# Second layer's weights split early and parked in DRAM, image product packed into one fp32r product, last batch closed in two parts, slot and opening order changed

## The chip, the cores and the metric

The kernel runs on one core of a Trainium2 chip. Five engines work side by side, each through its own instructions in order: TensorE (PE, with its weight loads PEld), VectorE (DVE), ScalarE (ACT), GpSimd (POOL) and SyncE (SP, which here only issues DMA transfers; ACT issues a few too). The metric is the device time of one execution in microseconds (us). Times of the runs are of the whole execution; the span in the profile goes from the first to the last instruction.

## The reference: what is computed

Two cross-attention layers on 16 sequences of 256 positions with 320 channels (20 heads of 16), against a context of 256 tokens with 512 channels. Everything is float32.

```python
def layer0(x, ctx):                       # text = first 77 tokens, ip = the other 179
    q, k, v = x @ Wq, text @ Wk, text @ Wv
    text_out = softmax(q_h @ k_h.T * scale) @ v_h
    ip_k, ip_v = ip @ Wk_ip, ip @ Wv_ip
    text_probs = softmax(q @ k.T * scale)              # over all channels
    sem = (text_probs @ text) @ ip.T * scale
    ip_probs = softmax(q_h @ ip_k_h.T * scale + 0.5 * sem) * spatial_mask
    return (text_out + ip_probs @ ip_v_h) @ Wout + bout + x

def layer1(x, ctx):                       # text = first 252 tokens, ip = the last 4
    q, k_t, v_t = heads(x @ W_q), heads(text @ W_k), heads(text @ W_v)
    probs_t = softmax(q @ k_t.T * scale)
    text_out = probs_t @ v_t
    qsem = l2norm(probs_t @ text)                      # one vector per head
    sem = qsem @ l2norm(ip).T
    probs_ip = softmax(q @ k_ip.T * scale + 0.5 * sem) * spatial_mask
    return (text_out + probs_ip @ v_ip) @ W_out + b_out + x
```

## The kernel before

**Numbers.** A matmul of fp32r operands (rounded floats) is one record in the profile, one of f32 operands is two. To keep float32 accuracy most operands are held as a high half (the rounded value, copied by ACT) and a low half (the rest, subtracted by DVE or POOL), made by `halves` (lines 187 and 188). `prod` (line 260) then adds high x high, high x low and low x high. A few products are plain f32.

**Slots.** Each layer has 80 slots: 16 batches with 5 groups of 4 heads. Slot k of layer 0 (`slot0`) computes transposed scores T for slot k, the plain scores S of slot k+2 (for the row maxima) and the weighted values of slot k-1; slot k of layer 1 (`slot1`, from slot 80 on) does the same through `both1` (lines 917 and 922), then the norms that `l2norm` needs, `norm1` (lines 975 to 980: a Gram matrix times the rounded probabilities, multiplied with the probabilities' parts on DVE and summed on DVE or POOL), for slot k-1, and the text values `attend1` (lines 988 and 990) for slot k-2, with the settling `settle1` (lines 1040 to 1048) that transposes and scales them.

The maximum of each query's scores goes in as one more row of the queries: DVE reduces (line 923), TensorE turns the maxima into a row (`maxima1`, line 955), ACT copies it (line 957) and issues a small DMA into the stacked queries `qs` (line 959).

**Pieces between.** Whatever is not tied to a slot (keys `k0`/`k1`, values, Gram matrices `t1`, queries `q0`/`o1`, the closing products `c0`/`c1`, the image softmax `i1`, the second layer's weights `w1` to `w8`) is a generator, called a task, and `STEPS` lists at which time, in slots relative to its batch, each of its steps is issued. `fill(now)` issues the steps that are due. `late` puts DVE work off while `hold` is on, until `release` or `settled`.

**Order.** What is issued in the opening (`begin`) and in layer 1 is kept in that order on all engines; in layer 0 that holds for TensorE, and the other engines' order comes from a scheduler; `queued` and `anchor` tie single instructions behind the slot's main ones.

**Stages** in the profile: loads and opening to about 82 us, layer 0 in its steady form to about 555, the transition (second layer's weights, first keys and queries of layer 1, last slots of layer 0) to about 700, layer 1 steady to about 1430, the end to 1476.5.

**Second layer's weights** (`weights7`, `weights6`, `weights2`, `weights4`): 20 parts are loaded into `rawc`, split by ACT and DVE into `wA`, `wB`, `wC`, `wE` and `wF`, all in the transition. `weights8` fills `spread_d`, a DRAM table from which each batch reads its image values `vb`.

**Image softmax and closing** (`image_softmax`, lines 1058 to 1100; `close1`): for a batch whose five groups have settled, small operations of POOL, DVE and ACT compute `probs_ip` for all heads at once into `pip`; DVE turns it into `pT` (line 1100); `close1` multiplies it with `vb` (line 1108, f32), adds the text part on DVE (line 1109), makes halves (`ho`), and `project` (line 632) multiplies with `W_out`. The last batch's image softmax is already cut once, groups 0 to 3 and group 4, but only before the turn.

## Time and profile before

| what | us |
|---|---|
| runs | 1479.34, 1482.8, 1478.5 (median 1479.34) |
| profiled execution | 1478.29 |
| its span | 1476.5 |
| layer 0, steady (157.4 to 555) | 397.6 |
| transition (555 to 700) | 145.0 |
| layer 1, steady (700 to 1430) | 730.0 |
| end (1430 to 1476.5) | 46.5 |

The mean granted TensorE clock is 0.992 of full speed. In the profile a row of the groups names line, engine, operation, the tile written and the tiles read, the shapes and the count, then busy time and mean duration in ns, then the idle time of the engine just before, with what ended it. A row of the waits says which engine at which line waited for which other: total, times, longest. A row of the chain of waits has start, length and what ran. A row of an issue has the shortest, median and longest duration in ns. PE is busy while a matmul is under way, so a busy PE isn't a PE without overlap.

### The profile page before, as it was taken

The page shows a single profiled execution, that of the slowest core. Times are in us where ns is not written, and L with a number is a line of the kernel's source. Part 1 is how long each engine was busy: PE and PEld are TensorE (multiplying, and loading weights), DVE is VectorE, ACT ScalarE, POOL GpSimd, SP SyncE. Part 2 cuts the span into 40 slices and gives each one's busy share as a digit, 9 for nine tenths or more (in the row PEclk, how much of TensorE's full clock was granted, in tenths as well). Part 3 has the DMA queues.
Part 4 walks back from the last instruction along what each step waited for, and adds up shares of the span by engine and source line. Part 5 has one row for each costly group of instructions (what it writes and reads, how often), then busy time and mean ns, then how long its engine had stood idle before and what let it go on. Part 6 is the DMA issues. An engine that isn't in the chain of part 4 may idle for free.

```text
span 1476.5 us, 35304 instructions
## 1 busy us (share of the span) xinstructions
PE 1431.7 (97%) x12438; PEld 1184.3 (80%) x12438; DVE 1167.9 (79%) x2569; ACT 955.8 (65%) x2074; POOL 1154.1 (78%) x1173
## 2 busy tenths in 40 slices
PE   6899999999999999899999999999999999999998
PEld 6788888888888878677778888888888888888865
DVE  5477776777767787977888888888888888888897
ACT  5567676767676776756666666656665666566563
POOL 5259797978787878987788878787778877887786
PEclk9899999999999999999999999999999999999999
DMA  6766666565656577665434433543454345434511
GB/s 198 170 171 178 149 158 165 152 167 147 170 151 170 149 187 215 146 184 163 135 107 140 147 117 102 161 146 102 119 161 143 93 130 160 133 100 120 150 31 50
DMA packets 230667, 211.78 MB, mean 143 GB/s; under 512 B 56314, under 2 KB 217116, under 8 KB 230492
## 3 DMA queue, kind: packets, MB, share of 16 engines
q1 hardware_dynamic: 229232, 208.57, 50.5%
q8 instruction: 99, 1.62, 0.5%
q10 hardware_dynamic: 1260, 0.97, 0.2%
q14 instruction: 76, 0.62, 0.1%
HBM read 122.07 MB, written 86.44 MB: 141 GB/s over the span
## 4 chain that ended last, share of the span: by engine, by line
PE 87%; DVE 5%; DMA 2%; ACT 2%; issue 2%; POOL 2%; SPq 1%; DVEq 0%; ACTq 0%; POOLq 0%
PE X L260 22%; PE X L975 17%; PE X L632 11%; PE P L833 7%; PE S L772 6%; PE P L988 5%; PE T L917 5%; PE T L795 5%; PE S L922 3%; PE P L990 2%; PE X L690 1%; PE X L1108 1%; POOL wt L966 1%; PE X L780 1%; SPq L83 1%
## 5 line engine op out<-in xcount | busy, mean ns | idle before, releaser
L801 POOL TENSOR_TENSOR P<-P,rs 128x512 f32<-128x512 f32 x320 | 414.4, 1319 | 142.2 <-ACT P L798 142.0
L975 PE MATMUL X<-ctb,gm 128*128 128x512 f32 x1120 | 292.2, 403 | 0.0
L966 POOL TENSOR_TENSOR wt<-P,ctb 128x512 f32<-128x512 f32 x212 | 268.5, 1295 | 0.0
L923 DVE TENSOR_REDUCE mn<-S 128x4 fp32r<-128x1008 f32 x160 | 192.8, 1205 | 80.3 <-PE S L922 78.5
L975 PEld LDWEIGHTS X<-ctb,gm 128*128 128x128 f32 x1120 | 201.2, 188 | 48.7 <-issue 0.4
L798 ACT ACTIVATE P<-T 128x512 f32<-128x512 f32 x320 | 174.7, 593 | 97.6 <-PE T L795 80.0
L978 DVE TENSOR_TENSOR wt<-X,wt 128x512 f32<-128x512 f32 x240 | 159.3, 680 | 4.0 <-PE X L975 3.4
L929 ACT ACTIVATE P<-T 128x512 f32<-128x512 f32 x212 | 115.0, 597 | 54.4 <-PE T L917 41.8
L980 POOL TENSOR_TENSOR wt<-wt 128x512 f32<-128x512 f32 x80 | 103.6, 1295 | 57.5 <-DVE wt L978 57.5
L774 DVE TENSOR_REDUCE mn<-S 128x4 fp32r<-128x716 f32 x160 | 142.4, 890 | 0.0
L965 ACT ACTIVATE ctb<-P 128x512 fp32r<-128x512 f32 x212 | 122.2, 625 | 30.4 <-PE X L975 29.2
L833 PE MATMUL P<-P,vr 128*32 128x256 f32 x1920 | 123.9, 389 | 0.6 <-DVE sp L693 0.6
L632 PE MATMUL X<-hq,wE 128*128 128x256 f32 x768 | 111.4, 290 | 4.9 <-ACT hq L615 3.6
L260 PE MATMUL X<-cta,wA 128*128 128x252 f32 (+3 forms) x726 | 104.9, 290 | 6.1 <-ACT wA L187 5.3
L632 PEld LDWEIGHTS X<-hq,wE 128*128 128x128 f32 x768 | 102.2, 196 | 7.6 <-ACT hq L615 4.0
L632 PE MATMUL X<-ho,wF 128*128 128x256 f32 x768 | 106.6, 285 | 0.9 <-DVE ho L871 0.6
L260 PEld LDWEIGHTS X<-cta,wA 128*128 128x128 f32 (+1 forms) x726 | 94.8, 191 | 10.2 <-ACT wA L187 5.6
L632 PEld LDWEIGHTS X<-ho,wF 128*128 128x128 f32 x768 | 98.7, 189 | 3.9 <-DVE ho L871 1.0
L844 DVE STREAM_TRANSPOSE nt<-P 128x512 f32<-128x512 f32 x80 | 57.1, 714 | 44.6 <-PE P L833 44.4
L833 PEld LDWEIGHTS P<-P,vr 128*32 128x32 f32 x1920 | 55.4, 111 | 41.4 <-issue 5.5
L773 DVE TENSOR_REDUCE mn<-S 128x4 fp32r<-128x308 f32 x160 | 74.4, 465 | 17.4 <-PE S L772 16.9
L917 PEld LDWEIGHTS T<-qs,ks 49*128 49x128 f32 x640 | 50.3, 184 | 46.5 <-issue 19.9
(223 smaller groups left out, 3319.6 us busy)
## 6 DMA issues: line engine op xcount, KB each, us to landing
qd<-q SPq DMA_DIRECT2D x48, 384.0 KB
kd<-kst SPq DMA_DIRECT2D x66, 256.0 KB
rawc<-in_cT_dram SPq DMA_DIRECT2D x60, 256.0 KB
qs<-qd SPq DMA_DIRECT2D x160, 96.0 KB
ks<-kd SPq DMA_DIRECT2D x160, 96.0 KB
qs<-qd SPq DMA_DIRECT2D x60, 192.0 KB
ks<-kd SPq DMA_DIRECT2D x60, 192.0 KB
qd<-q SPq DMA_DIRECT2D x32, 256.0 KB
```

What stands on the lines that cost most here:

```text
L260: last = mm(out, lhs(a, k), rhs(b, k), start=i == 0, stop=i == len(terms) - 1)
L632: mm(pp, w(s, k, slice(m * 128, (m + 1) * 128)), a[:, t], start=i == 0, stop=i == len(terms) - 1)
L774: anchor(nc.vector.tensor_reduce(mn[:, t, 1], sp[:, :, T0:], axis=AX.X, op=ALU.max))
L798: exp = anchor(nc.scalar.activation(pt, st[p], AF.Exp, scale=SCALE))
L801: anchor(nc.gpsimd.tensor_mul(pt, pt, rs[:, t : t + 1].to_broadcast([128, 2, S])))
L833: mm(pv[32 * s : 32 * s + 32, o : o + S], v[:, vt, h : h + 32], P[k, s // 2][:, t, s % 2], start=vt < 2, stop=vt != 1,)
L917: mm(st[u][:, j], c[1][rows, j, lo : lo + 128], c[0][rows, j], start=True, stop=True)
L923: anchor(nc.vector.tensor_reduce(maxes[k + 2][:, t], sp[:, :, :T1], axis=AX.X, op=ALU.max))
L965: nc.scalar.activation(R[k, u][:, t], P[k, u][:, t], AF.Copy, scale=0.5)
L966: anchor(nc.gpsimd.tensor_sub(W[k, u][:, t], P[k, u][:, t], f(R[k, u][:, t])))
L975: mm(yp, gm[:, gb], R[k, u][:, kt], start=i == 0, stop=i == len(blocks[n]) - 1)
L978: nc.vector.tensor_mul(product, yp, w[:, n])
```

## The change

1. *Weights parked.* A new task `prep` reads the 20 parts of the second layer's weights during layer 0 (slots 8.4 to 14.4 of each ten, 12 steps in ten slots), splits each (POOL copies, DVE subtracts) and stores both halves in DRAM (`parked`). In the transition the same steps only bring halves back, one DMA for a part.
2. *Packed image product.* `probs_ip` is packed as [high, low, high] and the image values as rows [high, high, low], so that one fp32r matmul with 128 rows gives what the f32 one gave. The image softmax has three more steps: high copies, low subtraction, three turns and three copies to `pT`. `vipd` has three parts, `spread_d` is ordered by position first, and its 24 fills carry three parts each.
3. *Order in a slot of layer 1.* The row of maxima is made right behind `both1(k, 1)`, for slot k+1, in the second half of the bank that holds the text sums; its DMA is issued at once. Late work is released after the first norm product and held again at once; the roundings `rounded1` move one place back. All `STEPS` of layer 1 differ.
4. *Last batch.* `close_first` closes groups 0 to 3 and starts the output product, `close_last` adds group 4 and writes the output in three transfers. In the last slot the norm parts are summed by TensorE (more `zone` matmuls) in place of the adds.
5. *Opening.* `begin` issues single steps in another order, and `opening` is the new slot 0; `queued` ties nothing before `begin` has ended.

```diff
     def queued(inst, *behind):
         for other in behind or [anchors.get(inst.ins.engine)]:
-            if other is not None:
+            if other is not None and begun:
...
+    def stored(name, w_d, kt, n, half=None, columns=False):
+        d = parked[name] = dram.tile([128, 2, kt, n], F32, name=f"parked_{name}")
...
+        for i, (part, hi, lo) in enumerate(parts):
...
+            dma(raw, part)
+            yield
+            queued(nc.gpsimd.tensor_copy(high.bitcast(FR), raw))
+            queued(nc.vector.tensor_sub(raw, raw, high))
+            if half is not None and i == 2:
+                queued(nc.vector.tensor_scalar_mul(raw, raw, half))
+            yield
+            dma(hi, high)
+            dma(lo, raw)
+            yield
...
+    def brought(parts):
+        for w, d in parts:
+            dma(w, d)
+            yield
...
     def weights7():
         cip = w1["cip"]
-        image, wki1 = by_column(wki1_d)
-        _, text, w1["k"] = by_row(wk1_d, "wA")
-        yield from in_turn(image + text, 0.3, "rawc")
+        image, wki1 = from_columns("ki")
+        text, w1["k"] = from_rows("k", "wA", 4, CP)
+        yield from brought(image + text)
...
-                    src = vipd.rearrange("(b n) c -> b n c", n=NIP)[:, :, lo : lo + 16]
-                    dma(spread_d[:, 32 * s + row : 32 * s + row + NIP, lo : lo + 16], src)
+                    dma(rows[s, :3, row : row + NIP * B, lo : lo + 16], table[:, :, lo : lo + 16])
...
-    def maxima1(k):
-        mn = maxes[k]
-        mp = bank()
+    def maxima1(k, bank):
         for t in range(2):
-            mm(mp[:4, t * 128 : (t + 1) * 128], mn[:, t], ident_r, start=True, stop=True)
+            mm(bank[:4, S + t * 128 : S + (t + 1) * 128], maxes[k][:, t], ident_r, start=True, stop=True)
         mt = buf("mt", [8, S], FR)[:4]
-        nc.scalar.copy(mt, mp[:4, :S])
+        nc.scalar.copy(mt, bank[:4, S:])
         row = QK[k][0].rearrange("(u p) j t -> u p j t", u=2)[:, XROW]
-        late(lambda: nc.scalar.dma_start(f(row), f(mt)))
+        nc.scalar.dma_start(f(row), f(mt))
...
         if k > NS + 1:
             yield lambda: summed.append(attend1(k - 2))
-        yield release
         yield lambda: both1(k, 1)
+        yield lambda: maxima(k + 1, summed)
         if last:
             yield lambda: norm1(last, 0, 0)
         yield 0.2
+        yield release
+        if mine:
+            yield hold
         for parts in summed:
             yield lambda: settle1(*parts)
         if last:
             yield lambda: norm1(last, 0, 1)
-        if mine:
-            yield lambda: rounded1(k, 0)
         yield 0.4
         if last:
             yield lambda: norm1(last, 1, 0)
-        yield 0.6
+        if mine:
+            yield lambda: rounded1(k, 0)
         if last:
             yield lambda: norm1(last, 1, 1)
-        if mine:
-            yield hold
+        yield 0.6
+        yield 0.8
+        yield lambda: stacks(k + LEAD)
         if mine:
             yield lambda: rounded1(k, 1)
-        yield 0.8
-        yield lambda: maxima(k + 2)
-        yield lambda: stacks(k + LEAD)
         yield 1.0
...
+        for d, x in pieces:
+            (nc.vector.tensor_copy if lo else nc.scalar.copy)(d[:, :, :, :8], x)
+            nc.scalar.copy(d[:, :, :, 16:24], x)
+        yield
+        for d, x in pieces:
+            pool.tensor_sub(d[:, :, :, 8:16], x, f(d[:, :, :, :8]))
+        yield
+        turned = w1["turned"]
+        for i in turns:
+            late(lambda i=i: nc.vector.transpose(turned[i], f(packed[i // 2][:, i % 2]).rearrange("p f c -> p (f c)")))
+        yield
+        settled()
+        for i in turns:
+            nc.scalar.copy(pT[i], turned[i])
         return pT, vb
+
+    def close_first():
...
+        for p in range(2):
+            row(p)
+            yield
...
+    def close_last():
...
+        for m, pp in enumerate(outs):
+            for s in range(2):
+                mm(pp, wo[1](s, 2, slice(m * 128, (m + 1) * 128)), hl[:, 2], start=False, stop=s == 1)
...
         def rows(p, hp):
-            mm(hp, bd[:, p * 128 : (p + 1) * 128], pT, start=True, stop=True)
+            mm(hp, bd[:, p * 128 : (p + 1) * 128], pT[p], start=True, stop=True)
             nc.vector.tensor_add(hp, hT[:, p], hp)
...
-        "k1": (-7, -6.2, -6.2, -5, -4.2, -3.4,),
-        "t1": (-3.2, -2.2, -2.2, -1.4, -0.2,),
-        "o1": (-7, -6.8, -6, -5.8, -4, -3.4,),
-        "i1": (6.8, 7.6, 7.6, 8.8, 9.4, 9.6, 10.6, 10.8, 10.8, 12.2,),
+        "k1": (-6.8, -5.8, -5.8, -5.2, -4.2, -3.2,),
+        "t1": (-2.6, -2, -1.2, -0.8, 0.6,),
+        "o1": (-6.8, -6.2, -5.4, -5.4, -4.6, -3.4,),
+        "i1": (7.4, 8, 8.2, 8.4, 10.2, 10.2, 10.8, 10.8, 10.8, 11.6, 12, 12.4, 12.4,),
         "c1": (12.8, 12.8, 13.4, 14, 14, 15.8,),
...
+    task(("prep",), [10 * (i // PREP) + 8.4 + 6.0 / PREP * (i % PREP) for i in range(60)], prepare)
...
     def begin():
-        parts = lambda *keys: [step(key) for key in keys if key in tasks]
-        k0, q0, s0, m0, q1 = ("k0", 0), ("q0", 0), ("s0", 0), ("m0t", 0), ("q0", 1)
-        parts(k0, k0, k0, q0, q0, q1, q0, q0, q0)
...
+        part("k0", 0)
+        part("q0", 0)
+        part("k0", 0)
...
+        score0(0, 0)
+        part("k0", 0)
+        part("v0", 1)
+        score0(0, 1)
+        part("v0", 1)
+        maxima0(0, nc.sync)
+        part("k0", 1)
...
+    def opening():
+        yield lambda: turned0(0, 1)
+        yield lambda: score0(2, 0)
...
```

278 lines of the change are left out of this document (206 added, 72 removed), and 35 rows, old and new, of the table STEPS.

## The prediction

> **What bounds the kernel now.** I read the page first, then a table of stretches, the chain of waits, the waits by line, and short timelines.
>
> ```profile
> span 1476.5 us, 35304 instructions
> PE 1431.7 (97%) x12438; PEld 1184.3 (80%) x12438; DVE 1167.9 (79%) x2569; ACT 955.8 (65%) x2074; POOL 1154.1 (78%) x1173
> ...
> PE 87%; DVE 5%; DMA 2%; ACT 2%; issue 2%; POOL 2%; SPq 1%; DVEq 0%; ACTq 0%; POOLq 0%
> ```
>
> TensorE is busy 97% and is 87% of the chain that ends last, so there are two ways to gain: less TensorE work, or fewer of its waits. The stretches say where the waits lie (columns: length; busy time of PE, its weight loads, DVE, ACT, POOL; granted clock; DMA share; GB/s).
>
> ```profile
> 48.70:81.45 32.75, 25.80 (x163) 22.36 (x161) 18.23 (x34) 13.62 (x33) 11.35 (x9) 0.79 0.54 148
> 157.40:555.00 397.60, 393.60 (x3717) 339.07 (x3709) 290.27 (x697) 288.46 (x624) 329.54 (x292) 1.00 0.62 160
> 555.00:700.00 145.00, 134.54 (x1267) 110.72 (x1267) 114.96 (x259) 96.09 (x207) 120.32 (x112) 0.99 0.64 178
> 603.90:608.60 4.70, 4.64 (x37) 2.56 (x37) 1.74 (x4) 4.09 (x9) 3.76 (x5) 0.64 0.16 44
> 700.00:1430.00 730.00, 727.27 (x6120) 585.05 (x6119) 626.55 (x1301) 455.43 (x985) 581.50 (x629) 1.00 0.42 126
> 1430.00:1476.50 46.50, 38.38 (x274) 27.39 (x274) 35.77 (x85) 17.73 (x41) 30.95 (x44) 0.99 0.16 47
> ```
>
> Busy time times clock is work at full clock. The late opening (48.7 to 81.45) holds 25.80 x 0.79 = 20.4 us of it, so 12.4 of its 32.75 us are lost. The transition loses 145 - 134.54 x 0.99 = 11.8, the end 46.5 - 38.38 x 0.99 = 8.5. Layer 0 (157 to 555) and steady layer 1 (700 to 1430) lose 4.0 and 2.7 in all: there only less TensorE work helps.
>
> **The change, part by part.**
>
> *Packed image product.* The product that adds the image tokens' part to a closed batch (line 1108) is f32 now and fp32r after, with three rows of high and low halves in place of one. A query or output product (line 632) is an fp32r matmul of the same 256 columns, so the price of the new form has a row.
>
> ```profile
> 1001.91 0.59 PE L1108 MATMUL X<-rs,rs 128*128 128x256 f32 x2
> ...
> 1042.51 1.02 PE L1108 MATMUL X<-rs,rs 128*128 128x256 f32 x4
> ```
>
> Those are two stretches of TensorE's timeline (start, length, records). The chain of waits has the fp32r groups beside them:
>
> ```profile
> 1000.26 1.81 PE X L975 x7
> ...
> 1005.65 2.91 PE X L632 x24
> ...
> 1039.22 3.45 PE X L975 x14
> ...
> 1043.54 3.16 PE X L260 x24
> ...
> 1049.90 1.82 PE X L975 x7
> ```
>
> Four records take 1.02 and two 0.59, so they start (1.02 - 0.59)/2 = 0.215 apart. One batch has 6 (3 products, two passes each): 1.29 us. Three fp32r matmuls at 2.91/24 = 0.121 are 0.36. Saved: 0.93 a batch, 14.8 over 16. Against it stand, per batch, two more transposes on DVE, seven small copies on ACT and two subtractions on POOL.
>
> ```profile
> L923 DVE TENSOR_REDUCE mn<-S 128x4 fp32r<-128x1008 f32 x148 | 178.4, 1206 | 77.3 <-PE S L922 75.4
> ...
> L978 DVE TENSOR_TENSOR wt<-X,wt 128x512 f32<-128x512 f32 x224 | 148.5, 680 | 1.2 <-PE X L975 0.8
> ...
> L980 DVE TENSOR_TENSOR wt<-wt,X 128x512 f32<-128x512 f32 x74 | 50.8, 687 | 2.5
> ...
> L939 DVE COPY sr<-S 128x16 f32<-128x16 f32 x148 | 24.2, 163 | 0.0
> ...
> L1040 DVE STREAM_TRANSPOSE nt<-P 128x256 f32<-128x256 f32 x74 | 32.5, 439 | 0.0
> ...
> L957 ACT CAST mt<-X 4x256 fp32r<-4x256 f32 x75 | 26.4, 352 | 0.3 <-PE X L955 0.3
> ...
> L895 DVE SCALAR_TENSOR_TENSOR xc<-X,bo,xc 128x256 f32<-128x256 f32 x40 | 18.0, 476 | 0.0
> ```
>
> A batch lasts 1049.90 - 1000.26 = 49.64. DVE is busy 626.55/730 of it, 42.6; with 2 x 0.439 it is 43.5 of 48.7. On the mean that is covered by idle time; in one slot it is not. Per batch the fillers are 84 key, value and Gram matmuls (3.16/24 = 0.132 each: 11.1), 48 query and output ones (5.8) and the 1.29, so the fixed part of a slot is (49.64 - 18.2)/5 = 6.3. The new times of the pieces (STEPS) leave one slot in five with 12 key matmuls alone: 6.3 + 1.6 = 7.9 us on TensorE. DVE needs there two reductions (2.41), two copies (0.33), four norm products (2.72), a sum (0.69), the settling transpose (0.44), and reciprocal, scaling and two further pieces, each between 0.16 and 0.48 by these rows (0.6 to 1.9): 7.2 to 8.5. So that slot is a tie, and behind it the late DVE work that is now released before the settling, not ahead of it, can hold a norm product's bank. Bounds for this loss: 0 (the bank ring and the next, longer slots take it up) and 2.7 us a batch (0.7 carried out of the short slot, 0.5 where ACT's copies stand behind the transposes and the exponentials behind them, 1.5 where three late pieces of 0.48 stand before the settling). I take 0.4, nearer to nothing, as DVE's mean slack is 5 us a batch. Layer 1: -14.8 + 16 x 0.4 = -8 (from -15 to +28).
>
> *Row of maxima (line 955 on).* The product that turns the maxima of a slot's scores into a row, and the small load that puts this row under the queries, come one slot later than before: in the middle of slot k for slot k+1, where it was at the end of slot k for k+2. T of slot k+1 (line 917) reads that row. Behind the second half of the scores ACT still has a pair of exponentials (2 x 0.6 us, the rounding of line 929), then the 0.352 copy, the issue and the landing:
>
> ```profile
> L929 ACT ACTIVATE P<-T 128x512 f32<-128x512 f32 x198 | 107.5, 596 | 49.1 <-PE T L917 36.6 <-PE S L922 11.4 <-ACT mt L957 0.6
> ...
> L959 ACTq DMA_DIRECT2D qs<-mt x80: 517/518/536, 669.8 to 1439.6; - x80
> ...
> 460.00 2.10 DMA kd<-kst
> ...
> 597.11 4.25 DMA rawc<-in_wvi_dram
> ```
>
> 1.2 + 0.35 + 0.52 + 2.1 (the lower of the two landings shown; this one has 4 KB, so that neither is nearer in kind, and it moves beside steady traffic as the keys of the 2.1 do) = 4.2. TensorE has 3.45 (14 norm matmuls) + 1.6 to do meanwhile in the short slot: 0.9 us to spare, more in the others. I take nothing; with a landing of 4.25 it would be 1.3 a batch. The product goes into the free half of the bank of the text sums, so that DVE's settling now also waits for ACT's copy, with that slot's norm products queued behind it: 1.2 + 0.35 after the scores, while DVE has the second reduction (1.21) and a late piece to do, so again nothing, and at most the 0.35 of the copy (inside the 2.7).
>
> *Second layer's weights.* 20 copies (ACT) and 20 subtractions (DVE) leave the transition; layer 0 takes them on POOL and DVE, with 40 stores.
>
> ```profile
> L188 DVE TENSOR_TENSOR wB<-rawc,wB 128x512 fp32r<-128x512 f32 x6 | 7.0, 1159 | 0.2 <-ACT wB L187 0.2
> ...
> L187 ACT CAST wB<-rawc 128x512 fp32r<-128x512 f32 x6 | 3.6, 623 | 1.4 <-DMA rawc<-in_wvi_dram 1.4
> ...
> L188 POOL TENSOR_TENSOR cta<-rawc,cta 128x512 fp32r<-128x512 f32 x6 | 7.7, 1294 | 0.0
> ...
> L801 POOL TENSOR_TENSOR P<-P,rs 128x512 f32<-128x512 f32 x320 | 414.4, 1319 | 142.2 <-ACT P L798 142.0
> ...
> PE X L709 <- ACT sp L705: 4.2, 2, 2.9
> ```
>
> In the transition 20 x at most 1.16 = 23 us leave DVE (115 of 145 busy) and 20 x at most 0.62 = 12 leave ACT. The costliest stall, 2.9 us at TensorE behind ACT, and the half clock behind it (0.64 over 603.9 to 608.6) start with the 4.25 us landing on which ACT's copy of wB blocks: that goes, since the halves land ready for TensorE and no engine stands between. Waits on DVE shrink; the one on spread_d below and those on POOL stay. Halves are twice the bytes, 8.2 MB in place of 4.1: 28 GB/s more beside 178. I take half of the 11.8 lost: -6 (from -10, little left, to +3, the larger loads late). In layer 0, a fifth of the stretch from 157 to 555 takes four parts: POOL 4 x at most 1.29 = 5.2 of (397.60 - 329.54)/5 = 13.6 idle, DVE 4 x 1.16 = 4.6 of 21.5. If each of 20 parts pushed a softmax product back by one such copy with no slack, 26; POOL's own idle before line 801, 142 us over 320, says it is nearer to 0: +1. SP's queue gets 60 more issues there; DMA's share is 0.62.
>
> *Opening.* The loads of contexts 2 and 3 are issued 18 places earlier on SP's queue, no longer behind the stack loads and the first maxima rows, and scores, weights and keys are interleaved anew.
>
> ```profile
> 55.66 2.32 issue
> ...
> 60.50 4.92 DMA raw<-in_cT_dram
> ...
> 67.78 3.10 DVE ctb L188 x2
> ```
>
> That load and the two splits behind it, 8.0 us of the chain, come off it; the next arrivals are the keys' round trip and the maxima, already 2.3 us of issue. I take -6 (from -12, all of the loss, to +3, a load now ahead of one that is needed sooner). The Trainium skill, "TensorE: Matmul & The Clock Gate", part 1, says that an idle window of about 3.4 us halves the clock. The row: at 603.9 an idle 2.9 did. By the page, gaps kept short would also return the clock's part, 25.80 x 0.21 = 5.4, which -12 would include; by the row it takes gaps below 2.9, and I leave -6.
>
> *End.* The last batch's image softmax goes in two parts, its output products of groups 0 to 3 are summed early, and the output leaves in three transfers.
>
> ```profile
> 1466.76 1.16 PEld L1108 LDWEIGHTS X<-rs,rs 128*128 128x128 f32 x6 [1.23 <-DVE rs L1100]
> ...
> 1469.17 3.13 PE L632 MATMUL X<-ho,wF 128*128 128x256 f32 x23 [0.40 <-DVE ho L871]
> ...
> 1472.86 0.38 SPq L83 DMA_DIRECT2D out_dram<-xq  x1
> ```
>
> Of the 3.13 only 6 of 24 matmuls stay (-2.3); the 1.23 wait is no longer for a whole transpose, and the last load leaves 1476.5 - 1472.86 = 3.6 us for 384 KB, now for 128. About -4 (from -6 to +1, small steps added to one serial chain).
>
> **Sum**: -6 + 1 - 6 - 8 - 4 = -23. The profiled execution is 1478.29 (span 1476.5 and 1.8 around it), 1.05 below the median: 1455.
>
> **Rivals.** (a) Everything comes: opening -12, transition -10, layer 1 -15, end -6, layer 0 none: -43, 1435. For it: steady layer 1 has almost no idle TensorE time, so work taken away there shows. Against: DVE in the short slot, and new first waits in opening and transition that nothing in this trace prices. (b) Layer 1's gain is hidden: DVE is the bound in the short slot and what TensorE saves is idle time there (0.93 lost of 0.93); the rest stands: -15, 1463. For it: 42.6 of 49.64 us of DVE work, and the shift of fillers out of that slot. (c) Maxima rows land in 4.25: 1.3 a batch, layer 1 -14.8 + 20.8 = +6, sum -9: 1469. For it: the slack of a whole slot is given up. Against: the row is 4 KB and has ACT's own queue. (d) The change doesn't do in the transition what it says, as the halves, twice the bytes, come late where the raw parts did (4.25 us), and the stores and splits delay layer 0 by a third of the 26 above: transition +3, layer 0 +8, sum -7: 1471. For it: SP's queue is in order and carries both. Against: DMA's share of 0.62 to 0.64. The Trainium skill, "DMA: Bandwidth & Descriptors", specifications, wants 512 B or more for line rate; the new spread_d fill has 24 x 192 pieces of 64 B in place of 24 x 64. The row below is one wait of TensorE behind it; by the page there would be more of them.
>
> ```profile
>   PE X L780: 1.4, 1
> ```
>
> (e) Slower: DVE's in-order queue. It is the queue of the slots behind the short one: late pieces now come ahead of the settling and of the sums that free a norm product's bank, and each delay is carried on as DVE has little slack until a slot of ten us or more. From 1.86 us a batch ((14.8 + 15)/16) this eats all; at 2.7 layer 1 is +28 and the time 1491. For it: 7.2 to 8.5 against 7.9; against: 5 us of slack a batch.
>
> **Chances.** Forecast 0.52 (own range 1444 to 1463); (a) 0.12, (b) 0.10, (c) 0.06, (d) 0.05, (e) 0.15. About 0.3%, 4.4 us, is what a measurement here can tell from none: (e) ends slower in most of its cases, so slower 0.13, same 0.04, faster 0.83. The range 1436 to 1477 leaves out (e) and the edge of (a).
>
> **What would show it.** Batches of 48.7 to 49.1 us in steady layer 1 (of 49.64); no TensorE wait on DVE products above 0.7 a batch; the T of line 917 not waiting for a DMA; transition of 139 and opening of 76; no fp32r weight subtraction in the transition; the last output issue 4 us earlier relative to the last zone sum. A batch above 50 us proves (e) or (c), by which engine the norm products or T wait for.

## The result, and the profile after

The changed kernel takes 1485.77 us (median of 20 runs, 1479.21 to 1490.33); the kernel before, on the same chip, 1481.45 (20 runs, 1476.83 to 1484.39). The ratio is 1.0026 with a 95% interval of 1.0015 to 1.0037: 4.3 us slower, about the 4.4 that the prediction took for the least a measurement can tell from none, where 1455 was predicted. The profiled execution took 1487.63 us, 1.9 above its median; that of before, 1478.29, lay 3.2 below the median of these runs. So the two traces lie 9.3 us apart where the medians lie 4.3 apart, and about 5 us of what follows is run to run.

The page of the changed kernel: span, busy time of the engines, chain of waits.

```profile
span 1485.8 us, 35473 instructions
PE 1424.2 (96%) x12410; PEld 1175.6 (79%) x12410; DVE 1177.1 (79%) x2607; ACT 960.8 (65%) x2167; POOL 1171.3 (79%) x1217
...
PE 76%; DVE 8%; DMA 6%; POOL 3%; issue 3%; ACT 3%; SPq 1%; ACTq 0%; DVEq 0%; POOLq 0%
```

TensorE is busy 7.5 us less (the packed product was priced at 14.8), but its part of the chain fell from 87% to 76%; DMA's rose from 2% to 6% and DVE's from 5% to 8%. So the lost time is waiting. The stretches (same columns as in the prediction) say where:

```profile
48.70:81.45 32.75, 27.06 (x208) 24.41 (x210) 19.72 (x41) 17.20 (x41) 11.13 (x9) 0.90 0.68 189
157.40:555.00 397.60, 389.82 (x3653) 335.46 (x3646) 296.92 (x700) 282.38 (x608) 338.24 (x307) 1.00 0.70 191
555.00:700.00 145.00, 128.03 (x1190) 104.94 (x1189) 99.49 (x233) 86.28 (x188) 112.81 (x108) 0.96 0.66 182
700.00:1430.00 730.00, 721.40 (x6137) 580.56 (x6136) 630.82 (x1325) 463.46 (x1078) 592.57 (x657) 1.00 0.43 128
1430.00:1485.80 55.80, 45.37 (x327) 31.17 (x325) 43.93 (x110) 27.36 (x71) 34.31 (x47) 0.99 0.15 46
```

The late opening is better: 27.06 x 0.90 = 24.4 us of full-clock work in the same 32.75 us, where it was 20.4. The transition is worse: 145 - 128.03 x 0.96 = 22.1 us lost, where it was 11.8. DMA's share of layer 0 went from 0.62 to 0.70.

Fixed stretches hold different work in two kernels, so a ledger by slots is better. Each slot has one reduction of its first half of scores on DVE (`mn<-S`), and its start marks the slot in every kernel. (A slot's scores S are computed two slots ahead of its exponentials, so the mark is early by about that much.) Two neighbouring slots of the changed kernel's timeline on DVE (start, length) show how the marks are read:

```profile
602.70 0.89 DVE L844 TENSOR_REDUCE mn<-S 128x4 fp32r<-128x716 f32 x1
605.61 0.89 DVE L844 TENSOR_REDUCE mn<-S 128x4 fp32r<-128x716 f32 x1
608.39 0.89 DVE L844 TENSOR_REDUCE mn<-S 128x4 fp32r<-128x716 f32 x1
618.75 0.89 DVE L844 TENSOR_REDUCE mn<-S 128x4 fp32r<-128x716 f32 x1
```

These are second and first halves in turn. 605.61 is the first half of slot 72 and 618.75 that of slot 73: 13.14 us where the kernel before has 7.15. The ledger, in us against the kernel before (its own marks in the second column; each column is one profiled execution; "1:0" is slot 0 of layer 1):

| slot | before | after | same kernel again | zero fill in old place | that, again | no parking | both |
|---|---|---|---|---|---|---|---|
| 5 | 94.9 | -5.9 | -4.3 | -5.4 | -7.4 | -6.5 | -5.3 |
| 60 | 508.4 | -0.9 | -0.7 | -1.7 | -1.2 | -5.5 | -4.3 |
| 70 | 591.5 | +2.0 | +3.7 | +2.7 | +5.1 | -5.4 | -2.7 |
| 75 | 624.7 | +6.6 | +7.5 | -0.4 | +2.0 | +0.1 | +3.0 |
| 1:0 | 662.4 | +9.9 | +8.9 | +4.3 | +7.9 | +2.1 | +6.2 |
| 1:15 | 799.2 | +13.0 | +11.9 | +4.6 | +11.3 | +8.1 | +14.0 |
| last | 1432.9 | +4.7 | +3.7 | -3.6 | +3.2 | -0.1 | +5.8 |
| end of span | 1476.5 | +9.3 | +8.3 | +2.1 | +7.5 | +3.8 | +10.0 |

(Labels from the fourth column on: changed_again, fill_first, fill_first_again, weights_back, fill_no_parking. The profile of weights_back lies 6.3 us below the median of its runs, the others within 3 of theirs.) Column "after" by stages: opening -5.9, layer 0 to slot 60 +5.0, from there to slot 15 of layer 1 +13.9, the rest of layer 1 -8.3, end +4.6. Two stages did what was forecast; three did not. The marks enclose nearly the same work: from slot 60 to slot 15 of layer 1 the traces hold 2500 matmul records of TensorE before and 2488 after, while its idle time there rose from 14.4 to 24.8 us and the mean granted clock fell from 0.994 to 0.972.

**The costliest wait.** The timeline of the changed kernel in slot 72 (start, length, records, idle time before and who ended it), with the queues' issues:

```profile
601.63 4.62 SPq L85 DMA_DIRECT2D spread_d<-kb  x4
...
605.14 0.62 ACTq L853 DMA_DIRECT2D qsl<-mt  x1
...
606.35 1.33 SPq L85 DMA_DIRECT2D ks<-kd  x1
...
607.72 1.27 SPq L85 DMA_DIRECT2D qs<-qd  x1
...
610.68 0.36 ACT L852 CAST mt<-X 8x256 fp32r<-8x256 f32 x1 [0.40 <-DMA qsl<-mt]
615.79 0.62 ACTq L853 DMA_DIRECT2D qs<-mt  x1
...
617.12 1.19 PE L842 MATMUL S<-ks,qs 125*128 125x256 f32 x4 [7.56 <-DMA qs<-qd]
```

The four fills of `spread_d` with zeros are 768 KB each. In the kernel before they left 45 us earlier, in slot 66 by the marks:

```profile
556.96 2.78 SPq L83 DMA_DIRECT2D spread_d<-kb  x3
561.17 1.30 SPq L83 DMA_DIRECT2D spread_d<-kb  x1
```

Cause: `packed` and `zero` are two buffers of one ring, taken in one line, and in the new code `zero` is the second one, which layer 0's last batch still uses until about 598. The load of stacked queries issued at 607.72 stands behind what is left of 3.1 MB: by the semaphores in the trace the four fills land at 606.7, 608.9, 611.0 and 614.3. The chain of waits of the changed kernel has it landing 9.27 us after its issue:

```profile
607.72 9.27 DMA qs<-qd
```

ACT is held too: its copy of the maxima ends at 611.04, and the small DMA behind it in ACT's own queue leaves at 615.79. What this issue waits for is not data. The transfers of this program, those of SP and of ACT together, take turns with eight semaphores that tell of their landing, and one is not issued before the last one with its semaphore has landed, about eight issues back. In the trace the issue at 615.79 waits for the semaphore of SP's load of stacked keys of 606.35, which lands at 615.71. TensorE stands 7.56 us. The windows of the same place:

```profile
605.00:610.00 5.00, 4.24 (x51) 3.00 (x50) 4.80 (x13) 4.94 (x11) 4.81 (x6) 1.00 1.03 365
610.00:615.00 5.00, 0.00 (x0) 0.00 (x0) 1.96 (x4) 0.64 (x2) 3.77 (x4) 0.90 1.04 274
615.00:620.00 5.00, 2.88 (x16) 2.68 (x20) 1.65 (x3) 1.09 (x2) 0.49 (x1) 0.50 0.74 138
```

All sixteen DMA engines are busy (share 1.03), TensorE does nothing for five us, and has half the clock in the next five. In slot 64 (10.72 us for 6.87) the halves do the same, on a smaller scale:

```profile
534.05 5.32 SPq L85 DMA_DIRECT2D wA<-parked_k  x3
...
544.39 0.63 ACTq L853 DMA_DIRECT2D qsl<-mt  x1
...
545.12 1.08 ACT L868 ACTIVATE P<-T 128x512 f32<-128x512 f32 x2 [4.40 <-DMA wA<-parked_k]
...
545.77 1.28 PE L865 MATMUL T<-qs,ks 127*128 127x256 f32 x4 [2.12 <-ACT P L868]
```

ACT's exponentials need no DMA. They stand behind ACT's own issue of the maxima row, and that waits for the semaphore of the last of wA's four loads, which is eight issues back. The chain of waits has it:

```profile
538.85 5.46 DMA wA<-parked_k
...
544.39 0.63 ACTq L853
...
545.12 0.61 ACT P L868
```

In the eighteen profiles ACT's issues were held over 0.5 us 198 times, and each time until the last transfer with the same semaphore had landed (0.1 us before the issue). The kernel before has one such hold, of 0.7 us; the changed kernel has 13, seven of them over 0.8 us and 20 us together. No run gave ACT's rows semaphores of their own.

### The profile page after: what moved, and what is told of

Its sections match the earlier page's. It is cut to its first block, busy times and chain, and to the rows that moved or that the text cites. A ratio compares the mean times of both kernels' runs of the same rounds, so it can differ in the third digit from the quotient of the medians.

```text
span 1485.8 us, 35473 instructions
## 1 busy us (share of the span) xinstructions
PE 1424.2 (96%) x12410; PEld 1175.6 (79%) x12410; DVE 1177.1 (79%) x2607; ACT 960.8 (65%) x2167; POOL 1171.3 (79%) x1217
## 4 chain that ended last, share of the span: by engine, by line
PE 76%; DVE 8%; DMA 6%; POOL 3%; issue 3%; ACT 3%; SPq 1%; ACTq 0%; DVEq 0%; POOLq 0%
PE X L310 19%; PE X L1045 16%; PE X L702 10%; PE P L903 6%; PE S L842 5%; PE T L865 4%; PE P L1058 4%; PE T L988 3%; PE S L993 3%; PE P L1062 2%; DMA kd<-kst 2%; DVE mn L994 1%; POOL P L871 1%; DMA qs<-qd 1%; PE P L1024 1%
## 5 line engine op out<-in xcount | busy, mean ns | idle before, releaser
L1045 PE MATMUL X<-ctb,gm 128*128 128x512 f32 x1120 | 287.6, 400 | 1.6 <-DVE hsn L1126 0.8
L1048 DVE TENSOR_TENSOR wt<-X,wt 128x512 f32<-128x512 f32 x241 | 162.4, 686 | 12.1 <-PE X L1045 9.1
L1034 ACT ACTIVATE ctb<-P 128x512 fp32r<-128x512 f32 x212 | 121.9, 628 | 11.9 <-PE X L1045 9.7
L702 PE MATMUL X<-hq,wE 128*128 128x256 f32 x768 | 107.7, 288 | 4.3 <-ACT hq L685 3.7
L702 PE MATMUL X<-ho,wF 128*128 128x256 f32 x744 | 102.0, 283 | 0.1
L702 PEld LDWEIGHTS X<-ho,wF 128*128 128x128 f32 x744 | 95.6, 190 | 2.7 <-DVE ho L942 0.4
L842 PE MATMUL S<-ks,qs 125*128 125x256 f32 x480 | 87.1, 304 | 8.5 <-DMA qs<-qd 7.6
L842 PEld LDWEIGHTS S<-ks,qs 125*128 125x128 f32 x480 | 65.5, 192 | 32.9 <-issue 23.1
```

Of the source, the lines that this page charges most:

```text
L702: mm(pp, w(s, k, slice(m * 128, (m + 1) * 128)), a[:, t], start=i == 0, stop=i == len(terms) - 1)
L842: mm(sp[:, h], Q[: XROW + T0, h, t * 128 : (t + 1) * 128], K[: XROW + T0, h], start=True, stop=True)
L1034: nc.scalar.activation(R[k, u][:, t], P[k, u][:, t], AF.Copy, scale=0.5)
L1045: mm(yp, gm[:, gb], R[k, u][:, kt], start=i == 0, stop=i == len(blocks[n]) - 1)
L1048: nc.vector.tensor_mul(product, yp, w[:, n])
```

## The experiments

Each kernel is compared with the kernel before on the same chip (medians of 1480.15 to 1481.82). Each starts from the changed kernel where nothing else is said.

**The fill moved early** (zero_early).

```diff
+        blank = buf("rawc", [128, 512], bufs=2, name="blank")[:, :CP]
+        nc.gpsimd.memset(blank, 0.0)
+        for b in range(0, B, 4):
+            dma(spread_d[:, b : b + 4], blank.unsqueeze(1).to_broadcast([128, 4, CP]))
...
-            dma(spread_d[:, b : b + 4], zero[:, :CP].unsqueeze(1).to_broadcast([128, 4, CP]))
```

> The changed kernel with one edit: spread_d (3.1 MB) is zeroed at slot 8 of layer 0 from another blank buffer, not in the transition. Theory: in the changed kernel the four zero fills are issued at 601.6 us right ahead of the stack loads of the next slots, and TensorE then waits 7.6 us for those loads; with the fills gone from there slot 72 takes about 7 us in place of 13.1, and the whole is about 6 us shorter (near 1480). Rival: it is the halves of the weights, brought in bursts, that fill the queue; then the wait only moves to another slot of the transition and the time stays within 2 us.

1487.53 us, ratio 1.0038 (1.0017 to 1.0059). The stall of slot 72 went (slots 70 to 75: from +4.6 to -3.1), but slots 10 to 15, where the 3.1 MB now lie, lost 9.4. The chain of waits there has a load of stacked keys that takes 7.78 us to land:

```profile
138.88 7.78 DMA ks<-kd
```

The window at that place shows TensorE busy for 2.67 us of 5 and all DMA engines busy:

```profile
140.00:145.00 5.00, 2.67 (x20) 2.43 (x21) 3.06 (x5) 2.80 (x5) 2.91 (x4) 1.00 1.10 349
```

So the stall goes with the bulk: apart from one memset no engine works for these four transfers, and a slot pays for them where the next slots' stacks stand behind them. The rival's time held, not its reason: the wait went to layer 0 and not to another slot of the transition.

**No parking** (weights_back): the weights are loaded and split in the transition as before, and all else is as changed. The times of the steps remain those made for the halves.

```diff
-    task(("prep",), [10 * (i // PREP) + 8.4 + 6.0 / PREP * (i % PREP) for i in range(60)], prepare)
...
-        image, wki1 = from_columns("ki")
-        text, w1["k"] = from_rows("k", "wA", 4, CP)
-        yield from brought(image + text)
+        image, wki1 = by_column(wki1_d)
+        _, text, w1["k"] = by_row(wk1_d, "wA")
+        yield from in_turn(image + text, 0.3, "rawc")
```

> The changed kernel with the first part undone: the second layer's weights are read and split in the transition, as before; nothing is parked in DRAM. Theory: the parking costs more than it brings. Layer 0 from slot 5 to 60 gets its 5 us back and slot 64 its 3.9 us (the loads of wA's halves in front of the stack loads): about 8 to 10 us shorter, near 1476. Rival, by the prediction: the halves save about 6 us of splitting in the transition, so undoing them costs that, less the 5 us of layer 0: about 1 us longer.

1488.43 us, 1.0039 (1.0016 to 1.0062). In layer 0 the opening's gain now stays flat at -5.5 from slot 15 to slot 70: parking costs 4.6 us to slot 60 and 3 more to slot 70. But the 5.5 are gone at slot 75, and 8 more at slot 15 of layer 1, so the time of the whole is the rival's. From slot 60 to slot 15 of layer 1 this kernel loses 13.6 us and the changed one 13.9: taking the halves out does not bring that stretch back.

**Old end** (end_back): old closing of the last batch, old order of the last slot and old times of its steps.

```diff
-ENDED = 2 * NS - 1
+ENDED = 9 * NS
...
-        ("i1", B - 1): (6.6, 6.6, 7, 7, 7, 7, 7, 7, 7, 7, 7, 7, 7,),
-        ("c1", B - 1): (7.2, 7.8,),
+        ("i1", B - 1): (6.8, 7.6, 7.8, 10, 10, 10, 11, 11, 11.2, 12, 12, 12, 12,),
+        ("c1", B - 1): (12.2, 13, 13, 13.2, 13.4, 16,),
```

> The changed kernel with the fourth part undone: the last batch is closed as before, in one piece after its group 4, with the packed product and one output transfer; the last slots' norm parts are added on POOL and DVE again. Theory: splitting the last entry costs the 4.6 us by which the end (from the last score reduction on) is longer than before, so this is 4 to 5 us shorter. Rival: that loss comes from the packing steps of the batches before the last one, which stand in slots without filler work, so the time stays within 1.5 us or gets longer by the 1.3 us that the part behind the last zone product gained.

1488.22 us, 1.0051 (1.0033 to 1.007). From the last mark to the end of the span: 43.6 us before, 48.2 after, 52.8 here. The fourth part as a whole saves 4.6, so the theory is refuted; the loss comes from elsewhere in the last slots.

**Image product in f32 again** (image_f32).

```diff
-            mm(hp, bd[:, p * 128 : (p + 1) * 128], pT[p], start=True, stop=True)
+            mm(hp, f(bd[:, p * 128 : (p + 1) * 128]), f(pT[p]), start=True, stop=True)
```

> The changed kernel with the image product of batches 0 to 14 as f32 matmuls of the same packed operands: all copies, subtractions and turns of the packing stay, only the three matmuls of each batch take two passes again. Theory: TensorE sets the pace of steady layer 1, so a batch takes 0.93 us longer (49.05 to 49.98), about 14 us in all. Rival: DVE in the short slot sets it; then it is less than 0.5 us a batch, under 7 us in all.

1500.05 us, 1.0119 (1.0094 to 1.0144): 14.3 more than the changed kernel. TensorE's timeline, first of the changed kernel, then of this one, in the same two places of a batch:

```profile
1005.37 0.39 PE L1247 MATMUL X<-kb,tph 128*128 128x256 f32 x2
1012.09 0.28 PE L1247 MATMUL X<-tph,tph 128*128 128x256 f32 x1
```

```profile
1007.50 1.02 PE L1247 MATMUL X<-kb,tph 128*128 128x256 f32 x4
1014.76 0.60 PE L1247 MATMUL X<-tph,tph 128*128 128x256 f32 x2
```

Two records take 0.39 us in place of four with 1.02, and one 0.28 in place of two with 0.60; two fp32r products lie 0.39 - 0.28 = 0.11 apart, where 0.121 was taken. The edit is in 15 batches: 14.3 us are 0.95 a batch (13.8 and 0.92 by the two ratios), and by the marks of slots 20 to 75 of layer 1 a batch takes 50.16 us beside 49.04, so 1.12; 0.93 was priced. Work taken from TensorE in steady layer 1 shows in full.

**The fill in its old place, by swapping the two buffers** (fill_first; again: fill_first_again).

```diff
-        packed, zero = [buf("kb", [128, 576], FR, bufs=2, name="packed")[:, : 2 * S] for i in range(2)]
+        zero, packed = [buf("kb", [128, 576], FR, bufs=2, name="packed")[:, : 2 * S] for i in range(2)]
```

> The changed kernel with two names swapped in weights8: the zeros for spread_d stand in the buffer kb that comes free first (batch 14's keys) and the packed values in the other. Theory: the change had made the fill's source the buffer that batch 15 uses last, so the fill moved from 557 us, in front of long TensorE groups, to 601 us, in front of the stack loads of slots 73 on. Swapped back, it lands near 560, slot 72 takes about 6 us in place of 13.1, and the time is 6 us shorter than the changed kernel's. Rival: the zeroed bytes cost the same 7 to 9 us wherever they stand, as when they were zeroed in layer 0; then slots 63 to 67 get that much longer and the whole stays.

> The kernel with the zero fill of spread_d in its old place, once more as it was (one blank line added). It says how far the earlier figure (1483.39, 1.0014 of before, interval 0.9987 to 1.0041) holds: theory, 1.000 to 1.003 again; rival (the earlier one was luck and the fill is worth nothing in the median): 1.003 to 1.005 as the changed kernel.

1483.39 us, 1.0014 (0.9987 to 1.0041), and 1484.34, 1.0006 (0.9984 to 1.0027). In both profiles slots 70 to 75 take 3.1 us less than before the change in place of 4.6 more. The window that held the stall in the changed kernel, here:

```profile
610.00:615.00 5.00, 4.35 (x42) 2.91 (x43) 4.33 (x11) 2.87 (x7) 5.00 (x6) 1.00 0.61 139
```

TensorE is busy 4.35 us of 5 at full clock. In its old place the fill is not free: slots 65 to 70 lose 2.1 and 2.3 us with it there, 0.1 in the changed kernel. Of the 7.7 us only about 2 are in the medians (mean ratio 1.0010 beside 1.0022 of the two takes of the changed kernel, and the intervals overlap). Other waits on transfers come five slots later, ACT's exponentials again, in fill_first:

```profile
642.28 1.08 ACT L868 ACTIVATE P<-T 128x512 f32<-128x512 f32 x2 [4.13 <-DMA ks<-kd]
...
648.83 1.09 ACT L868 ACTIVATE P<-T 128x512 f32<-128x512 f32 x2 [2.32 <-DMA spread_d<-vipd]
```

The two takes, with the same code, also differ by 5.4 us at the end of the span. From slot 60 to slot 15 of layer 1 alone they differ by 6.2: TensorE is idle 18.9 and 21.1 us there, and the mean granted clock is 0.989 and 0.972.

**The changed kernel once more** (changed_again; one blank line added).

> The changed kernel as it is, once more, beside the others on their chip. All theories: 1483 to 1488 at the median, slot 72 again over 11 us, slot 158 again over 10 us; where a stretch differs from the first profile by more than 2 us, that stretch varies from execution to execution and no verdict of one profile may rest on it.

1483.89 us, 1.0019 (0.9998 to 1.004). The ledger comes back within 1.7 us in each row.

**Last slots.** All of these start from fill_first. fill_first_steady_end takes the special times of batch 13 out. own_times starts the image softmax of batch 14 later, so that it does not force the last steps of batch 13. own_times_own_bank also gives the maxima of the last slots a bank of their own. early13 instead gives batch 13 earlier times. The cuts stand in this order:

```diff
-        ("i1", B - 3): (7.6, 8.2, 8.8, 8.8, 10.4, 10.4, 11.2, 11.2, 11.2, 12.6, 12.6, 12.6, 12.8,),
...
-        ("i1", B - 2): (7.2, 7.2, 7.6, 8.4, 8.4, 8.6, 9, 9, 9, 9.2, 9.4, 10, 10.6,),
+        ("i1", B - 2): (7.8, 7.8, 7.8, 8.4, 8.4, 8.6, 9, 9, 9, 9.2, 9.4, 10, 10.6,),
...
-            maxima1(k, pv[0][2] if pv else bank())
+            maxima1(k, pv[0][2] if pv and k < 2 * NS - 3 else bank())
...
-        ("i1", B - 3): (7.6, 8.2, 8.8, 8.8, 10.4, 10.4, 11.2, 11.2, 11.2, 12.6, 12.6, 12.6, 12.8,),
+        ("i1", B - 3): (7.4, 8, 8.2, 8.4, 9.4, 9.4, 10, 10.2, 10.4, 10.8, 11.2, 11.6, 11.6,),
```

> As the run with the fill first, and the image softmax and closing of batch 13 keep the times of the steady batches (their own rows of STEPS are gone). Theory: the 5.7 us of slot 158 come from the packing of batch 13, whose four copies, two subtractions and three turns stand in one slot that has no filler on TensorE, in front of the exponentials on ACT and of the norm products on DVE; a slot earlier there is filler to cover them, and slot 158 shrinks by 2 to 4 us. Rival: the end is long because of the new order in the slot; then the pieces' times change it by less than 1 us.

> As the run with the fill first, and the image softmax of batch 14 begins at 7.8, not 7.2, slots behind its base. At 157.2 its first step called for the result of batch 13's, and so forced that one's last four steps (four copies, two subtractions, three turns, three copies) together into the place ahead of slot 157's settling, though their own times are 157.6 and 157.8. Theory: that clump is what makes the text sums of slot 158 wait 2.2 us and the slot 11.2 us long; at their own times slot 158 is 2 to 3 us shorter and so is the end. Rival: the maxima's copy in the bank of the text sums is what delays; then slot 158 keeps over 10.5 us.

> As the run with batch 13's steps at their own times, and in the last three slots the row of maxima goes to a bank of its own (as before the change) and not into the bank of the text sums. Theory that the settling waits for ACT's copy there: slot 158 loses another 1 to 1.5 us. Rival, by the prediction, which priced that wait at nothing: no change beyond 0.5 us.

> Edit beside the old place of the zero fill: the image softmax of batch 13 gets earlier times, so that its last four steps are issued at 155.4 to 156.6 and not in a clump at 157.2, and its closing starts at 157. Theory (the 5.7 us of the end are the clump of image steps ahead of slot 157's settling): slots 157 and 158 go back by 3 to 5 us, end part (last maximum to the end) from 48.2 to 43 to 45. Rival (the slots are bound by the sum of small steps on DVE, ACT and POOL, of which the last three batches have more than before, not by their order): the same us appear in slots 155 to 157; last slots together within 1 us.

| kernel | us | ratio (interval) | last mark to end (before: 43.6, after: 48.2) |
|---|---|---|---|
| fill_first_steady_end | 1484.15 | 1.0013 (0.999 to 1.0036) | 49.4 |
| own_times | 1485.96 | 1.0042 (1.0023 to 1.0062) | 52.5 |
| own_times_own_bank | 1488.3 | 1.005 (1.0031 to 1.0069) | 52.8 |
| early13 | 1490.42 | 1.0064 (1.0044 to 1.0083) | 48.7 |

None shortens the end. The clump only moves. In early13 slot 158 takes 11.87 us from mark to mark, where it takes 8.47 in the kernel before and 7.90 in the changed one, and the waits of TensorE by line say why:

```profile
PE X L1247 <- ACT kb L1197: 3.7, 1, 3.7
```

The packed product of a batch closed earlier stands behind ACT's copies, and these behind DVE's turns. So the theory of a clump in front of one settling is refuted; the bank for the maxima is not it either.

**Pacing the halves** (fill_first_paced; from fill_first): a half is not issued ahead of the stack loads of its own slot.

```diff
         for w, d in parts:
-            dma(w, d)
+            load_ = nc.sync.dma_start(f(w), d)
+            if loads:
+                queued(load_, loads[-1])
             yield
```

> As the run with the fill first, and each load of a parked half is kept behind the stack loads of the slot in which its step stands, so that the loads come one or two a slot and not four in a row. Theory: bursts in front of the stack loads are what costs; slots 63 to 67 lose no more than 1 us against the kernel before (2.8 in the changed kernel), and the whole is 2 to 4 us shorter than with the fill alone. Rival: it is the number of bytes, not their bunching; then there is no difference beyond 1 us.

1486.38 us, 1.0038 (1.0012 to 1.0063). The stall of slot 64 goes, as the theory had it, but not its 2 to 4 us; slots 66, 77 and 79 lose 3.0, 5.9 and 3.3. The waits by line, ACT's exponentials:

```profile
ACT P L871 <- DMA ks<-kd: 6.0, 1, 6.0
```

**Parking spread out** (prep_spread; with the own bank, from fill_first): steps every 0.8 slots in place of bursts of 12 half a slot apart.

```diff
-    task(("prep",), [10 * (i // PREP) + 8.4 + 6.0 / PREP * (i % PREP) for i in range(60)], prepare)
+    task(("prep",), [8.4 + 0.8 * i for i in range(60)], prepare)
```

> As the run with the fill first, with the 60 steps of the parking spread evenly (one each 0.8 slots, over slots 8 to 56) in place of 12 in six of each ten slots, and the row of maxima in its own bank in the last three slots. Theory: what layer 0 loses (3.7 to 5.0 us from slot 5 to slot 60 in four profiles; none with the parking taken out) comes where the parking's loads and stores stand ahead of a keys', queries' or stack transfer; spread, they hit the tight slots too, so 2 to 5 us stay. Rival: it is their bunching, and spread evenly they cost under 1 us. In the last slots: alone the bank gives at most 1.5 us.

1497.34 us, 1.011 (1.0074 to 1.0146). With this edit the output is no longer the reference's, so it is no kernel to use; the transfers and splits are as many as before the edit, and only where the slots stand is read from it. From slot 5 to slot 60 it loses 13.1 us, the changed kernel 5.0: spreading made it worse.

**The small fills on ACT's queue** (fills_on_act; from own_times).

```diff
-                    dma(rows[s, :3, row : row + NIP * B, lo : lo + 16], table[:, :, lo : lo + 16])
+                    nc.scalar.dma_start(rows[s, :3, row : row + NIP * B, lo : lo + 16], table[:, :, lo : lo + 16])
```

> As the run with batch 13's steps at their own times, and the 24 small fills of spread_d (192 pieces of 64 B each) are issued by ACT, not by SP. Theory: slots 77 to 79 lose 5 to 6 us against before because the stack loads stand behind those fills in SP's queue and ACT's own small load of the maxima row, and the exponentials behind it, wait for them (4.1 us on ks<-kd at 642 us); off SP's queue the stack loads go first and the three slots give back 3 to 5 us. Rival: the pieces themselves fill the DMA engines; then the waits stay, and ACT loses 12 us of issue on top: 0 to 5 us longer.

1495.48 us, 1.01 (1.007 to 1.013). Slots 75 to 80 lose nothing, as the theory had it, but the next ten lose 13.5. TensorE's waits there:

```profile
PE T L988 <- ACT qsl L1000: 4.1, 1, 4.1
```

**Fill in its old place and no parking; the same with early13** (fill_no_parking, early13_no_parking).

> Edit: the zero fill of spread_d in its old place, and no parking (the second layer's weights loaded and split in the transition as before the change); all else as changed. Theory (parking in layer 0 and the moved fill are the two causes that eat the opening's gain): layer 0 keeps the opening's 5.5 us flat from slot 5 to slot 70, nothing is lost between slots 70 and 75 (5.5 were with the parking alone taken out), so first slot of layer 1 near -5 against before, steady layer 1 gains its 8, and even with the 5.7 us lost at the end the whole is 4 to 8 us faster than before: 1473 to 1477. Rival (the split itself in the transition costs what the halves' arrival cost, and the new times of layer 1's first pieces lose in its first 15 slots whatever stands before them): 5 to 9 us lost between slots 75 and 95 as in the kernel with the parking alone taken out; total no faster than before, 1479 to 1485.

> Both edits together with no parking: fill in its old place, weights split in the transition, earlier image softmax of batch 13. Sum of the first theory's parts: -5 (layer 0) - 8 (layer 1) + 1 (end) = -12, 1468. Rival: 5 to 9 lost in the first 15 slots of layer 1 and 5.7 at the end, 1480 to 1485.

1488.86 us, 1.0047 (1.0028 to 1.0066), and 1493.31, 1.0083 (1.0053 to 1.0114): the theory is refuted in both, and both take longer than even the rival said (at most 1485). Layer 0 keeps its gain, but slots 70 to 1:15 lose 16.7 us (the same order with halves: 1.9 and 6.2, fill_first and its second take). TensorE's waits between 588 and 668 us of fill_no_parking:

```profile
PE X L843 <- DVE mn L837: 3.9, 2, 2.8
PE X L772 <- ACT sp L768: 3.2, 1, 3.2
PE S L986 <- DMA ks<-kd: 2.3, 1, 2.3
```

The first two are DVE and ACT with the splits in their queues; the 3.2 is the old 2.9 behind ACT's `sp`. In the changed kernel neither is there. With the fill in its old place, parking is worth 10 to 15 us from slot 70 to 1:15 and costs 5.5 to 10 from slot 5 to slot 70. With the late fill (the two profiles of the changed kernel beside weights_back) it is worth 2.5 and 5.3 and costs 6.8 and 6.9. The medians (1488.86 beside 1484.34, 1488.43 beside 1485.77) say that it pays on the whole, with intervals that lie apart only in the first pair. How the splits would do with step times of their own in the new order was not tried.

## Why the prediction was wrong, by its steps

- **Opening, -6.** Right: -5.9 at slot 5, and -4.2 to -7.4 over all seventeen profiles that have it. The clock of the late opening rose from 0.79 to 0.90. The load of `raw` and the two splits behind it are no longer in the chain of waits, and the keys' round trip is (7.75 us from 44.70 and 2.74 from 67.18), as forecast.
- **Packed product and layer 1, -8.** Right, and for its reasons. From slot 20 to slot 75 eleven batches take 1400.7 - 861.3 = 539.4 us, 49.04 each, beside 546.6 and 49.69: 0.65 saved of 0.93, so the loss is 0.28 a batch where 0.4 was taken. The number predicted was 48.7 to 49.1. The ledger's -8.3 begins at slot 15; over all 80 slots, with the first 15, layer 1 gains 5.2. ACT does stand behind the transposes, much longer than the 0.5 taken, but beside other work. The waits by line of the changed kernel over the steady layer 1:

```profile
ACT kb L1197 <- DVE rs L1193: 42.8, 13, 3.5
```

  That is 3.3 us a batch at ACT, and TensorE sees none of it there; at the end of the kernel, with the fillers gone, the same pair stops TensorE for 3.7 us (early13 above).
- **Row of maxima, nothing.** Right. T's matmuls (line 988) wait 0.4 us for it, once, in the last slots, and in the steady part only its weight loads do, 1.1 us in two places; rival (c) falls. The shared bank was priced at nothing as well, and own_times_own_bank, which undoes it in the last three slots, found nothing.
- **Layer 0, +1.** Measured +5.0. The step priced POOL's and DVE's copies alone. The three kernels without parking lose 1.0 to 1.8 from slot 5 to slot 60, the twelve with it as written 2.4 to 6.2, so the parking is the cause. Whether it is the splits or the 60 transfers was not separated; zero_early shows that transfers alone can do it (9.4 us for 3.1 MB), DMA's share rose to 0.70, and ACT's issue at 395.66 in the changed kernel was held 2.67 us by the semaphore of a parking store.
- **Transition, -6.** The step that failed: +13.9, with the first 15 slots of layer 1 (10.8 up to their start). The halves were costed as an average, "28 GB/s more beside 178", and DMA's share of 0.64 was read as room. But they come as pieces of 320 to 512 KB in the queue that also brings the stacks of the next slots, which are issued just in time; for some microseconds the share is 1.0, and ACT's issue of the maxima row waits for their semaphores and stops ACT. Slots 64, 72, 77 and 78 lose 3.9, 6.0, 2.8 and 2.0 us, together 14.7. Nor was the fill of `spread_d` with zeros priced, as its lines look unchanged: the order of two names in one line moved it by 45 us, into the most crowded place. Slots 70 to 75 alone make 4.6 of the 13.9. Within the step, the forecast that ACT's 2.9 us at `sp` and DVE's splits go was right: neither is among the waits of the changed kernel, and both come back in fill_no_parking.

  The single stalls are shown by the runs that remove them; the whole is not. From slot 60 to 1:15 the four profiles with halves and the late fill lose 10.4 to 13.9 (mean 11.8), the six with halves and the fill in its old place 5.9 to 15.5 (mean 9.7; fill_first, its second take and the four of the last slots), zero_early 5.8, the three without halves 13.6 to 18.3 (mean 15.7). So in the mean the late fill explains about 2, the halves do beat the splits in this order of steps, and no version loses less than 5.8. What all share is the new order and the new times of the steps around the start of layer 1, which the sum put at nothing; only rival (a) named "new first waits in opening and transition that nothing in this trace prices". No run goes back to the old order there, so this rival stays open.
- Rival (d) had the place and the mechanism, large loads late, and a price of +3 where +13.9 came. The 24 small fills, of which it spoke, hold ACT up for 2.32 us in fill_first (its issue waits for the semaphore of one of them) where they held TensorE up for 1.4 before.
- **End, -4.** Measured +4.6. Behind the last zone product the changed kernel is shorter by 1.4 (14.5 us for 15.9). But the last slots now take the end of batch 13's image softmax, its closing and batch 14's image softmax in closer order. ACT's timeline, first of the changed kernel, then of before, has the first exponentials of slots 158 and 159:

```profile
1444.62 0.57 ACT L1000 ACTIVATE qsl<-T 128x512 f32<-128x512 f32 x1
...
1455.84 2.04 ACT L1000 ACTIVATE P<-T 128x512 f32<-128x512 f32 x4
```

```profile
1440.61 0.61 ACT L929 ACTIVATE qsl<-T 128x512 f32<-128x512 f32 x1
...
1446.07 1.09 ACT L929 ACTIVATE P<-T 128x512 f32<-128x512 f32 x2 [1.10 <-PE T L917]
```

  11.2 us pass where it were 5.5, and the difference, 5.7, is the whole of 4.6 + 1.4 but for 0.3. Two waits of TensorE in the changed kernel about there:

```profile
1444.75 1.21 PE L1062 MATMUL P<-wt,zone 128*32 128x256 f32 x8 [2.21 <-POOL wt L1050]
1449.45 0.93 PE L1045 MATMUL X<-ctb,gm 128*128 128x512 f32 x3 [0.82 <-DVE hsn L1126]
```

  The first wait ends with POOL's sum of products that DVE makes; it lies ahead of the 11.2 us. Inside them the chain of waits leaves TensorE and goes through norm products on DVE, the settling (`nt<-P`), more norm products and then the closing (`X`, `ho`):

```profile
1447.69 0.69 DVE wt L1048
1448.38 0.36 DVE nt L1122
...
1449.91 0.67 DVE X L1248 x2
...
1451.60 0.38 ACT ho L951
...
1452.01 0.49 DVE ho L944
...
1452.55 1.44 PE X L702 x10
```

  These are 4.9 us, from 1447.65 to 1452.55; the chain of the kernel before stays on TensorE from 1440.20 to 1446.04 (norm products, output products, T).

  The step saw what leaves the serial tail and not what the last slots get in exchange. This chain has the look of rival (e)'s mechanism, in two slots and not in steady layer 1, where it was placed. But four other orders did not get the time back, so which of these pieces costs it stays open.
- **Slots 75 to 1:15** are part of the transition's 13.9: they lose 4 to 9 us in the table's profiles with halves, and 8.0 and 11.0 without parking. In slot 91 TensorE waits for DVE's reductions (2.3 us longer than before in fill_first); part of it may be steps that now come later in the first batches. Not settled.

No version tried beats the kernel before; with the fill in its old place (1.0014 and 1.0006) the two are the same within what can be measured.

## What to carry to other kernels

A mean DMA share of 0.6 was no room for bulk here: ask what stands behind each large transfer in its queue, how many microseconds it has until it is needed, and which engine issues a small DMA that has to wait for it, be it only because both raise the same semaphore. When lines of an order change, look up every buffer of a ring again, also those whose own code is the same; here two names in one line moved 3 MB by 45 us. And when work is taken out of a serial tail, add it to the slots that receive it: here these lost more than the tail gained.

## What the runs showed of the hardware

A queue of one's own protected little here, for two reasons that the traces tell apart. First, transfers were slow in both queues: behind four fills of 768 KB on SP's queue the load of a stack (192 KB at most) took 9.27 us to land, and the row of 8 KB that ACT issued at 605.14 landed only at 610.61, 5.5 us later, where the median of such rows in this trace is 2.6. The Trainium skill, "DMA: Bandwidth & Descriptors", "Issuing engines are not separate DMA queues", says that transfers issued by different engines run on the same 16 DMA engines and interleave; here all are busy (a share of 1.03, 365 GB/s) while SP's load and ACT's row of 605.14 are both late, which agrees; how two queues share them no run here shows. Second, ACT stood 4.75 us (611.04 to 615.79) before its next issue, because that transfer was to raise the semaphore of a load in SP's queue that had not landed; this comes from how the program hands out its eight semaphores.

After TensorE's 7.56 idle us the granted clock was 0.50 over the next five. After the 2.12 idle us of slot 64 it was 0.50 from 545.77 to 549.18: a shorter gap than the 2.9 us from which the prediction read what halves the clock.
